# Cross-attention on one Trainium2 core: the output product with the output weights stationary and 512 tokens moving

## The chip, the cores and the metric

The kernel runs on one core of a Trainium2 chip, in one launch. The metric is device time in microseconds (us) of that launch: the median of three runs. The kernel's instructions go to five engines, each working through a queue of its own in the order in which the program writes them: PE (matrix products; its weight loads are listed as PEld), DVE (VectorE), ACT (ScalarE), POOL (GpSimd) and SP (SyncE), which here issues nearly all DMA transfers.

## The reference: what is computed

Inputs are x (32 batches, 512 tokens, 640 channels), a context of 32 x 77 x 1024, and weights. With 77 context tokens the object, other and image parts of the context are empty, so what is left is one cross attention with 20 heads of 32 channels, an output product, a bias and the residual:

```python
q = _heads(hidden_states @ to_q_w)                       # 32 x 20 x 512 x 32
h_txt = _sdpa(q, _heads(ehs_txt @ to_k_w), _heads(ehs_txt @ to_v_w))
out = _merge(h_txt)                                      # 32 x 512 x 640
out = out @ to_out_w + to_out_b
out = (out + residual) / RESCALE                         # residual = x, RESCALE = 1
```

All is float32. The kernel makes its big products in a rounded float32 form, each operand split into a high and a low part and three of the four partial products kept (PAIRS, line 113).

## The kernel before, in words

**Stages.** Up to about 250 us keys and values of all batches are computed from the context and written to scratch in device memory (lines 258 to 360). After that the kernel runs 160 *slots* (slot, line 588), one for each batch b and each chunk j of 128 channels (four heads): n = 5b + j. A slot has, among other work:

- scores(n): 32 small matmuls from qt (the queries, copied out of the bank pq) and kb (keys) into four banks sc, line 423;
- maxima(n) on DVE (line 435), exps(n) on ACT (line 445), normalize(n): a reciprocal on DVE (line 455) and a product on POOL (line 457), all on the probabilities pn;
- transpose_p(n - 1) on DVE (line 464), which turns pn in blocks of 32 into the tile z, and move_p, four DMAs on SP's queue that put z into raw with keys on the partitions (line 473). There are two buffers each of pn, z, qt and raw;
- queries(n + 1): 15 matmuls with wq_s stationary and 512 tokens moving (line 401), and copy_q, which puts the result into qt (line 410; on DVE in the slots below 7, on ACT from then on);
- values(m): 8 matmuls from raw and vb (line 483), then high_a on ACT (line 497) and low_a on DVE (line 502), which split the result into the tile at, one for each slot, eight buffers plus three borrowed ones;
- transpose_x on DVE (line 235) in chunks j = 0 and 1, two pieces each, and split_x on ACT and POOL (lines 245 and 246) in chunks 2 and 3, both for the next batch.

From slot 8 on (PAIRED) the slots differ by parity. An even slot, here called *paired*, computes values for two earlier slots at its end and issues a move_p behind them; an odd slot computes none, and issues its move_p in its middle, behind transpose_p. So two moves follow each other within a paired and the next unpaired slot.

**The output product.** For a batch, the projection goes over four blocks of 128 tokens (t), two halves of 320 output channels (h) and five chunks j: STEPS, 40 steps of three matmuls (project, line 521). The stationary operand is the piece at[tokens], 128 x 128, and the moving one is 320 columns of the output weights wo_s. Each (t, h) fills one PSUM bank po, which DVE adds onto the residual row tile xr (finish, line 550); there is one bank po. PIECES (line 565) spreads the steps of a batch over five slots, 7 to 10 steps in each: one part right after the scores, ahead of the queries, and one after the queries. The residual rows xr (128 tokens x 640 channels) are loaded by load_residual (line 509) and get the bias on POOL (add_bias, line 513); after both halves they go out (lines 554 and 556).

**The order.** manual_schedule (line 249) keeps, on each engine and on SP's queue, the order in which the program emits instructions; the framework adds waits where tiles are reused or read. An instruction that waits holds up everything behind it on its engine. In slot, for DVE, this order is: maxima, low_a, finish, transpose_p(n - 1), transpose_x, the reciprocal of normalize, finish. In the slots 1, 2, 5 and 6 transpose_p comes right behind maxima (line 606), and copy_q stands behind it on DVE (line 639); in the slots 3 and 4 transpose_p stands behind copy_q (line 640).

Of the kernel before, what the change touches and what calls it, by code (L numbers as in the profile page):

```python
# [23 lines left out]
P = 128  # L24
# [13 lines left out]
def kernel(  # L38
# [66 lines left out]

    def split_weights(dst, w, k, scale=None):
# [4 lines left out]
        split(dst[:, 0, :], dst[:, 1, :], part)  # L111

# [184 lines left out]
    def split_wo():  # L297
        k = len(split_ks) - NC_
        split_ks.append(k)
        ws = kvw.tile([P, 2, C], FPR, tag="ws", name="ws", bufs=2)  # L300
        split_weights(ws, wo, k)
        nc.sync.dma_start(wo_dram[:, k].bitcast(F32), ws.bitcast(F32))
# [73 lines left out]
    nc.sync.dma_start(bias, bo.unsqueeze(0).to_broadcast([P, C]))  # L376
    kbs = [main.tile([P, NC_, NKEY], F32, name=f"kb{n}") for n in range(2)]
# [31 lines left out]
    def copy_q(n, copy=nc.scalar.copy):  # L409
        copy(qts[n % 2], pqs.pop(n))  # L410

    def scores(n):
        b, j = divmod(n, NC_)
        scs[n] = [
            late[1].tile([P, NQ, P], F32, tag=LENT[n][i], name="sc", bufs=1 + (LENT[n][i] == "pa"))
            if i in LENT.get(n, ())
            else ps.tile([P, NQ, P], F32, tag="sc", name="sc", bufs=4)
            for i in range(HPC)
        ]
        for t in range(NQ):  # L420
            for i, sc in enumerate(scs[n]):
                r = slice(i * HD, (i + 1) * HD)
                nc.tensor.matmul(  # L423
                    sc[:, t, :NKEY],
                    qts[n % 2][r, t * P : (t + 1) * P],
                    kbs[b % 2][r, j, :],
                    start=True,
                    stop=True,
                    tile_position=(i * HD, 0),
                )  # L430
# [30 lines left out]
    def transpose_p(n):  # L461

        pn, z = pnb[n % 2], zs[n % 2]
        nc.vector.transpose(  # L464
            z.rearrange("p c h t j -> p (h t) c j"),
            pn.rearrange("p a (c i) -> p a c i", i=Q),
        )

    def move_p(n):

        raws[n] = late[0].tile([KPAD, NQ, HPC, P], F32, tag="raw", name="raw", bufs=2)
        for a in range(4):
            nc.sync.dma_start(  # L473
                raws[n][:, a].rearrange("p h q -> p (h q)"),
                zs[n % 2][a * Q : (a + 1) * Q].rearrange("i c h t j -> i c (h t j)"),
            )
# [15 lines left out]
    def high_a(n):  # L492
        if n % 11 < 8:
            at = late[0].tile([P, 2, S], FPR, tag="at", name="at", bufs=8)
        else:
# [9 lines left out]

    def load_residual(b, t, xr=None):
        if xr is None:
            xr = late[0].tile([P, C], F32, tag="xr", name="xr", bufs=4)
        nc.sync.dma_start(xr, x[b, t * P : (t + 1) * P, :])
        xrs[b, t] = xr  # L510

    def add_bias(b, t):
        nc.gpsimd.tensor_tensor(xrs[b, t], xrs[b, t], bias, ALU.add)  # L513

    def output_bank(b, t, h):
        if (b, h) == (B - 2, 0) and t > 0:
            pos[b, t, h] = ps.tile([P, S], F32, tag="pq", name="po", bufs=1)
        else:
            pos[b, t, h] = late[1].tile([P, S], F32, tag="po", name="po", bufs=1)

    def project(b, t, h, j):
        for m, (a, c) in enumerate(PAIRS):
            nc.tensor.matmul(  # L523
                pos[b, t, h][:, :HALF],
                ats[b * NC_ + j][:, a, t * P : (t + 1) * P],
                wos[0][:, j, c, h * HALF : (h + 1) * HALF],
                start=(j == 0 and m == 0),
                stop=(j == NC_ - 1 and m == 2),
            )

    STEPS = [(t, h, j) for t in range(NQ) for h in range(2) for j in range(NC_)]
    closed = []

    def piece(b, lo, hi):
        for t, h, j in STEPS[lo:hi]:
            if j == 0:
                output_bank(b, t, h)
            project(b, t, h, j)  # L540
            if j == NC_ - 1:
                closed.append((b, t, h))

    def finish():

        while closed:
            b, t, h = closed.pop(0)
            xr = xrs[b, t]
            cols = slice(h * HALF, (h + 1) * HALF)
            nc.vector.tensor_tensor(  # L550
                xr[:, cols], pos.pop((b, t, h))[:, :HALF], xr[:, cols], ALU.add
            )
            if (b, t) == (B - 1, NQ - 1):
                nc.sync.dma_start(out[b, t * P : (t + 1) * P, cols], xr[:, cols])
            elif h == 1:
                nc.sync.dma_start(out[b, t * P : (t + 1) * P, :], xr)

# [6 lines left out]

    PIECES = {
        2: ((2, 35, 40), (1, 0, 3)),
        3: ((1, 3, 5), (1, 5, 10)),
        4: ((1, 10, 15), (1, 15, 18)),
        0: ((2, 18, 20), (2, 20, 25)),
        1: ((2, 25, 30), (2, 30, 35)),  # L570
    }
    RESIDUAL = {1: (1, 0), 2: (1, 1), 4: (1, 2), 0: (2, 3)}
    BIAS = {2: (1, 0), 3: (1, 1), 0: (2, 2), 1: (2, 3)}
    TRANSPOSE_X = {0: (0, 1), 1: (2, 3)}
# [13 lines left out]
    def slot(n, beside=()):  # L588
        b, j = divmod(n, NC_)
        ahead, more = n + 1 < N, b + 1 < B  # L590
        pieces = [(b - back, lo, hi) for back, lo, hi in PIECES[j]]
        filling = n < NC_ + 2
# [23 lines left out]
        if b and j and b + 2 < B:  # L616
            load_x(b + 2, (j - 1,))
        if j in RESIDUAL and b >= RESIDUAL[j][0]:
            load_residual(b - RESIDUAL[j][0], RESIDUAL[j][1])
        if j in BIAS and b >= BIAS[j][0]:  # L620
            add_bias(b - BIAS[j][0], BIAS[j][1])
# [49 lines left out]
        if n == PAIRED - 1:  # L671
            move_p(n - 1)
        finish()
        if paired:
            move_p(n - 1)

    def end():


        last = B - 1  # L680
        load_residual(last - 1, 3)
        add_bias(last - 1, 2)
        add_bias(last - 1, 3)
        piece(last - 1, 18, 20)
        take(N - 3)
        finish()
        load_residual(last, 0)
        load_residual(last, 1)
        piece(last - 1, 20, 25)
        finish()  # L690
        transpose_p(N - 1)
        move_p(N - 1)
        piece(last - 1, 25, 30)
        finish()
        take(N - 2)
        piece(last - 1, 30, 35)
        finish()
        load_residual(last, 2)
        piece(last - 1, 35, 40)
        finish()  # L700
        for t in (0, 1, 2):
            add_bias(last, t)

        def begin(i, j0, j1):
            t, h = divmod(i, 2)
            if j0 == 0:
                if i < 4:
                    pos[last, t, h] = ps.tile([P, S], F32, tag="sc", name="po", bufs=4)
                elif i == 4:
                    pos[last, t, h] = ps.tile([P, S], F32, tag="pq", name="po", bufs=1)  # L710
                elif i == 5:
                    output_bank(last, t, h)
                else:
                    pos[last, t, h] = late[1].tile([P, S], F32, tag="pa", name="po", bufs=2)
            for j in range(j0, j1):
                project(last, t, h, j)

        for i in range(4):
            begin(i, 0, 4)
        take(N - 1)  # L720
        load_residual(last, 3)
        add_bias(last, 3)
        for i in (4, 5):
            begin(i, 0, 4)

        def close(t):
            for h in range(2):
                project(last, t, h, 4)
                closed.append((last, t, h))
            finish()  # L730

        close(0)
        close(1)
        begin(6, 0, 4)
        close(2)
        begin(7, 0, 4)
        close(3)
# [65 lines left out]
```

## Time and profile before

| what | value |
|---|---|
| time, median of 3 runs | 1742.69 us (1742.63 to 1742.89) |
| the profiled execution's own time | 1742.87 us |
| its span, first to last instruction | 1741.1 us |
| PE busy | 1732.8 us (100%) |
| DVE, ACT, POOL busy | 974.0, 1122.0, 788.9 us (56, 64, 45%) |
| time of the SP queue's packets, share of 16 DMA engines | 69.2% |
| granted TensorE clock | 1.0 |

The rows that the prediction shows come from one profiled execution. The page gives totals and the costliest groups of instructions (line, engine, operation, what it writes and reads, count, busy time, mean duration in ns, idle time before it). The timeline lists instructions in order of time with runs of the same kind merged: start, duration, engine, line, shapes, count, and in brackets the idle time of the engine before it with what ended it. A matmul's end is modelled, and matmuls overlap in the pipeline, so that spacing is read from one start to the next.

### The profile page before, as it was taken

What the parts mean: (1) busy time and instruction counts of PE and PEld (TensorE: products, weight loads), DVE (VectorE), ACT (ScalarE), POOL (GpSimd) and SP (SyncE); (2) the same over time, 40 slices, a digit from 0 to 9 for tenths busy, and PEclk for the clock granted to TensorE, in tenths of its full rate; (3) what the DMA queues carried; (4) which work ended last, traced back from release to release, by engine and by line L of the source; (5) the groups of instructions that cost most, each with busy time, mean ns of one, the idle gap of its engine ahead of it and who ended that gap; (6) DMA issues with size and microseconds to landing.
All of it is one profiled execution on the core that took longest, in us unless ns stands there. A gap on an engine that the chain in (4) does not pass through costs nothing.

```text
span 1741.1 us, 39488 instructions
## 1 busy us (share of the span) xinstructions
PE 1732.8 (100%) x13862; PEld 1434.1 (82%) x13862; DVE 974.0 (56%) x1651; ACT 1122.0 (64%) x5698; POOL 788.9 (45%) x502
## 2 busy tenths in 40 slices
PE   9999999999999999999999999999999999999999
PEld 7888898788888888888888888888888888888887
DVE  5342235656566565665666656656566566655653
ACT  3131126877777777777777777777777777777772
POOL 0000026555545545555455554555545555555443
PEclk9999999999999999999999999999999999999999
DMA  9847576877677676776776767767677677776655
GB/s 186 159 92 185 109 144 166 202 174 196 170 194 189 174 188 177 192 193 171 194 187 170 197 170 187 193 168 194 175 185 198 163 194 184 180 189 176 164 156 161
DMA packets 268567, 306.60 MB, mean 176 GB/s; under 512 B 88720, under 2 KB 165008, under 8 KB 268368
## 3 DMA queue, kind: packets, MB, share of 16 engines
q1 hardware_dynamic: 265776, 296.94, 69.2%
q0 software_dynamic: 2496, 6.97, 1.3%
q8 instruction: 110, 1.80, 0.4%
q14 instruction: 89, 0.73, 0.1%
q10 hardware_dynamic: 96, 0.16, 0.0%
HBM read 120.27 MB, written 57.88 MB: 102 GB/s over the span
## 4 chain that ended last, share of the span: by engine, by line
PE 98%; ACT 1%; DMA 1%; DVE 0%; issue 0%; SPq 0%; DVEq 0%; ACTq 0%
PE po L523 33%; PE pq L401 31%; PE sc L423 10%; PE pa L483 8%; PE pv L177 8%; PE pk L177 8%; DMA raw<-z 1%; ACT pn L445 1%; PE warm L256 0%; DVE z L464 0%; SPq L473 0%; DVE qt L410 0%; DVE nm L435 0%; DVE xr L550 0%; DVE zero L253 0%
## 5 line engine op out<-in xcount | busy, mean ns | idle before, releaser
L445 ACT ACTIVATE pn<-sc,nm 128x77 f32<-128x77 f32 x2560 | 788.1, 362 | 239.1 <-DVE nm L435 194.1
L457 POOL TENSOR_TENSOR pn<-pn,rs 128x1232 f32<-128x1232 f32 x160 | 363.4, 2271 | 689.1 <-DVE rs L455 682.8
L523 PE MATMUL po<-wo_s,at 128*128 128x320 f32 x3840 | 628.3, 313 | 0.0
L445 ACT ACTIVATION_READ_ACCUMULATOR pn<-sc,nm 128x1 f32 x2560 | 621.9, 243 | 0.0
L523 PEld LDWEIGHTS po<-wo_s,at 128*128 128x128 f32 x3840 | 575.3, 188 | 26.7 <-issue 2.5
L401 PE MATMUL pq<-xt,wq_s 128*128 128x512 f32 x2355 | 564.8, 391 | 0.0
L401 PEld LDWEIGHTS pq<-xt,wq_s 128*128 128x128 f32 x2355 | 435.4, 188 | 84.1
L435 DVE TENSOR_REDUCE nm<-sc 128x4 f32<-128x308 f32 x640 | 261.4, 471 | 137.0 <-PE sc L423 137.0
L464 DVE STREAM_TRANSPOSE z<-pn 128x1536 f32<-128x1536 f32 x160 | 283.0, 1769 | 0.7 <-DMA raw<-z 0.5
L423 PEld LDWEIGHTS sc<-kb,qt 32*128 32x128 f32 x5120 | 157.3, 186 | 85.4 <-ACT at L497 63.7
L550 DVE TENSOR_TENSOR xr<-po,xr 128x320 f32<-128x320 f32 x256 | 124.8, 489 | 167.8 <-PE po L523 146.5
L246 POOL TENSOR_TENSOR xt<-xs,xt 128x512 fp32r<-128x512 f32 x157 | 198.0, 1286 | 35.1 <-ACT xt L245 35.1
L513 POOL TENSOR_TENSOR xr<-xr,bias 128x640 f32<-128x640 f32 x128 | 200.4, 1566 | 13.2 <-DMA xr<-in_x_dram 11.1
L502 DVE TENSOR_TENSOR at<-pa,at 128x512 fp32r<-128x512 f32 x160 | 109.8, 686 | 148.2 <-ACT at L497 148.2
L497 ACT CAST at<-pa 128x512 fp32r<-128x512 f32 x160 | 94.1, 588 | 140.2 <-PE pa L483 138.9
L423 PE MATMUL sc<-kb,qt 32*128 32x77 f32 x5120 | 180.9, 277 | 2.2 <-DVE qt L410 1.4
L483 PE MATMUL pa<-raw,vb 96*32 96x512 f32 x1280 | 154.7, 599 | 0.8 <-DMA raw<-z 0.8
L177 PE MATMUL pv<-ct,wv_s 128*128 128x512 f32 (+1 forms) x600 | 133.9, 381 | 0.0
L177 PE MATMUL pk<-ct,wk_s 128*128 128x512 f32 (+1 forms) x600 | 133.4, 381 | 0.0
L177 PEld LDWEIGHTS pv<-ct,wv_s 128*128 128x128 f32 x600 | 112.5, 188 | 19.1
L177 PEld LDWEIGHTS pk<-ct,wk_s 128*128 128x128 f32 x600 | 112.4, 188 | 19.2 <-DVE wk_s L90 0.4
L410 ACT COPY qt<-pq 128x512 f32<-128x512 f32 x153 | 95.4, 623 | 31.1 <-PE pq L401 31.1
(35 smaller groups left out, 490.6 us busy)
## 6 DMA issues: line engine op xcount, KB each, us to landing
raw<-z SPq DMA_DIRECT2D x640, 192.0 KB, 3.5
xs<-in_x_dram SPq DMA_DIRECT2D x128, 320.0 KB, 5.3
xr<-in_x_dram SPq DMA_DIRECT2D x128, 320.0 KB, 5.0
out_dram<-xr SPq DMA_DIRECT2D x127, 320.0 KB, 4.2
vb<-v_dram SPq DMA_DIRECT2D x32, 240.0 KB, 4.6
kb<-k_dram SPq DMA_DIRECT2D x32, 192.5 KB, 3.9
cs<-in_ctx_dram SPq DMA_DIRECT2D x12, 512.0 KB, 9.3
k_dram<-ks POOLq DMA_DIRECT2D x20, 256.0 KB, 2.5
```

The source lines that it names most:

```text
L177: nc.tensor.matmul(held[j][:, :gn], w[:, k, a, :], cts[g, k][:, c, :gn], start=(k == 0 and n == 0), stop=(k == NK - 1 and n == 2),)
L246: low.tensor_tensor(parts[1], src, parts[0].bitcast(F32), ALU.subtract)
L401: nc.tensor.matmul(pqs[n], wq_s[:, k, a, j * P : (j + 1) * P], xts[b, k][:, c, :], start=(k == 0 and m == 0), stop=(k == NC_ - 1 and m == 2),)
L423: nc.tensor.matmul(sc[:, t, :NKEY], qts[n % 2][r, t * P : (t + 1) * P], kbs[b % 2][r, j, :], start=True, stop=True, tile_position=(i * HD, 0),
L435: nc.vector.tensor_reduce(nms[n][:, i], sc[:, :, :NKEY], AX.X, ALU.max, negate=True)
L445: nc.scalar.activation(pnb[n % 2][:, at, :NKEY], sc[:, t, :NKEY], AF.Exp, bias=nms[n][:, i, t : t + 1], accum_out=sms[n][:, at : at + 1],)
L457: nc.gpsimd.tensor_tensor(pf, pf, rs.unsqueeze(2).to_broadcast([P, NQ * HPC, NKEY]), ALU.mult)
L464: nc.vector.transpose(z.rearrange("p c h t j -> p (h t) c j"), pn.rearrange("p a (c i) -> p a c i", i=Q),)
L483: nc.tensor.matmul(pas[n][i * HD : (i + 1) * HD, :].rearrange("p (a q) -> p a q", q=P), vb[:, i, :], raw[:, :, i, :], start=True, stop=Tru ...
L513: nc.gpsimd.tensor_tensor(xrs[b, t], xrs[b, t], bias, ALU.add)
L523: nc.tensor.matmul(pos[b, t, h][:, :HALF], ats[b * NC_ + j][:, a, t * P : (t + 1) * P], wos[0][:, j, c, h * HALF : (h + 1) * HALF], start= ...
L550: nc.vector.tensor_tensor(xr[:, cols], pos.pop((b, t, h))[:, :HALF], xr[:, cols], ALU.add)
```

## The change

The output product of all batches but the last is turned round. Its stationary operand is a piece of wo_s, 128 x 128, and its moving operand is at with all 512 tokens (group). One group makes a block c of 128 output channels for 512 tokens: 15 matmuls of 512 columns in one whole bank. A batch has five groups, and GROUP puts one into each slot: nine matmuls after the scores, six after the queries. The columns of wo are permuted when it is split (turned=True), so that VectorE's transpose in blocks of 32 (turn) turns a bank into the layout in which x is loaded for the queries: partition = (channel quarter, token in 32), free = (token block, channel). POOL then adds the turned block ot onto the tile y (add). y holds x of a whole batch in that layout, loaded in quarters (load_y, LOAD_Y) and given the bias on POOL in four pieces (bias_of, with bias_y); two buffers. It goes out in the same layout, in pieces of 160 channels, that is 640 bytes (store_y, STORE_Y). The last batch keeps the old form on rows, with its own load_residual, project and finish.

For room, z and qt have one buffer instead of two, and at seven plus three instead of eight plus three. slot keeps its order otherwise. The core of the diff:

```diff
-    qts = [main.tile([P, S], F32, name=f"qt{n}") for n in range(2)]
-    zs = [main.tile([P, KBLK, HPC, NQ, Q], F32, name=f"z{n}") for n in range(2)]
+    qt = main.tile([P, S], F32, name="qt")
+    z = main.tile([P, KBLK, HPC, NQ, Q], F32, name="z")
...
+    def load_y(b, quarters):
+        if b not in ys:
+            ys[b] = late[0].tile([P, S // Q, U], F32, tag="y", name="y", bufs=2)
+        src = x[b].rearrange("(a j) (q u) -> q j a u", j=Q, q=4)
+        for q in quarters:
+            nc.sync.dma_start(ys[b][q * Q : (q + 1) * Q], src[q])
+
+    def bias_of(b, i):
+        part = ys[b][:, 4 * i : 4 * i + 4]
+        nc.gpsimd.tensor_tensor(
+            part, part, bias_y.unsqueeze(1).to_broadcast([P, 4, U]), ALU.add
+        )
+
+    def store_y(b, quarters):
+        dst = out[b].rearrange("(a j) (q u) -> q j a u", j=Q, q=4)
+        for q in quarters:
+            nc.sync.dma_start(dst[q], ys[b][q * Q : (q + 1) * Q])
...
+    def group(b, c, ks, tag="po"):
+
+        for k in ks:
+            if k == 0:
+                pos[b, c] = bank(tag)
+            for m, (a, d) in enumerate(PAIRS):
+                nc.tensor.matmul(
+                    pos[b, c],
+                    wos[0][:, k, a, c * P : (c + 1) * P],
+                    ats[b * NC_ + k][:, d, :],
+                    start=(k == 0 and m == 0),
+                    stop=(k == NC_ - 1 and m == 2),
+                )
+
+    def turn(b, c):
+        ots[b, c] = late[0].tile([P, S], F32, tag="ot", name="ot", bufs=1)
+        nc.vector.transpose(ots[b, c], pos.pop((b, c)))
+
+    def add(b, c):
+        part = ys[b][:, :, c * Q : (c + 1) * Q]
+        nc.gpsimd.tensor_tensor(
+            part, part, ots.pop((b, c)).rearrange("p (a i) -> p a i", i=Q), ALU.add
+        )
...
+    GROUP = {3: (1, 0), 4: (1, 1), 0: (2, 2), 1: (2, 3), 2: (2, 4)}
+    LOAD_Y = {0: (0,), 1: (1,), 2: (2, 3)}
+    BIAS = {4: (1, (0, 1)), 0: (2, (2,)), 1: (2, (3,))}
+    STORE_Y = {3: (0, 1), 4: (2, 3)}
...
-        if pieces[0][0] >= 0:
-            piece(*pieces[0])
+        if og >= 0:
+            group(og, oc, range(3))
         for i in range(2):
             exps(n, i)
-        finish()
         if not filling:
             transpose_p(n - 1)
         if n >= LATE and n != PAIRED - 1 and not paired and not copied:
             move_p(n - 1)
+        if j in STORE_Y and b > 1:
+            store_y(b - 2, STORE_Y[j])
...
-        if pieces[1][0] >= 0:
-            piece(*pieces[1])
+        if og >= 0:
+            group(og, oc, range(3, NC_))
+            turn(og, oc)
...
-        finish()
+        if og >= 0:
+            add(og, oc)
```

In end, the groups c = 2, 3 and 4 of the last batch but one are computed between the remaining values, two of them in the bank pq.

More of the change, by code (lines that the diff above doesn't have):

```diff
@@ L110, in split_weights @@
             nc.scalar.mul(part, part, scale)
-        split(dst[:, 0, :], dst[:, 1, :], part)
+        hi, lo = dst[:, 0, :], dst[:, 1, :]
+        if turned:
+            part = part.rearrange("p (q c i) -> p c q i", q=4, i=Q)
+            hi, lo = (d.rearrange("p (c q i) -> p c q i", q=4, i=Q) for d in (hi, lo))
+        split(hi, lo, part)
     PAIRS = ((0, 0), (0, 1), (1, 0))
@@ L376 @@
     nc.sync.dma_start(bias, bo.unsqueeze(0).to_broadcast([P, C]))
+    U = C // 4
+    bias_y = main.tile([P, U], F32, name="bias_y")
+    for q in range(4):
+        nc.sync.dma_start(
+            bias_y[q * Q : (q + 1) * Q, :],
+            bo[q * U : (q + 1) * U].unsqueeze(0).to_broadcast([Q, U]),
+        )
     kbs = [main.tile([P, NC_, NKEY], F32, name=f"kb{n}") for n in range(2)]
@@ L461, in transpose_p @@
     def transpose_p(n):
[L463 removed]
+        pn = pnb[n % 2]
         nc.vector.transpose(
@@ L504, in low_a @@
         )
[L506 to L528, printed above, removed]
-            )
[L533 to L556, printed above, removed]
+    ys, ots = {}, {}
@@ new lines, in bank @@
+    def bank(tag):
+        pool, bufs = (ps, {"sc": 4, "pq": 1}[tag]) if tag in ("sc", "pq") else (late[1], {"po": 1, "pa": 2}[tag])
+        return pool.tile([P, S], F32, tag=tag, name="po", bufs=bufs)
+    def group(b, c, ks, tag="po"):
[10 more added lines that the diff above has]
+                )
@@ new lines, in turn, with load_residual @@
+    def turn(b, c):
[5 more added lines that the diff above has]
+            part, part, ots.pop((b, c)).rearrange("p (a i) -> p a i", i=Q), ALU.add
+        )
+    def load_residual(t):
+        if B - 1 not in ys:
+            ys[B - 1] = late[0].tile([P, S // Q, U], F32, tag="y", name="y", bufs=2)
+        rows = ys[B - 1].rearrange("p a u -> p (a u)")
+        xrs[t] = rows[:, t * C : (t + 1) * C]
+        nc.sync.dma_start(xrs[t], x[B - 1, t * P : (t + 1) * P, :])
@@ new lines, in add_bias, with project @@
+    def add_bias(t):
+        nc.gpsimd.tensor_tensor(xrs[t], xrs[t], bias, ALU.add)
+    def project(t, h, k):
+        for m, (a, d) in enumerate(PAIRS):
+            w = wos[0][:, k, d].rearrange("p (c w) -> p c w", c=NC_)
+            nc.tensor.matmul(
+                pos[t, h][:, :HALF].rearrange("p (c w) -> p c w", c=NC_),
+                ats[(B - 1) * NC_ + k][:, a, t * P : (t + 1) * P],
+                w[:, :, 2 * h * Q : 2 * (h + 1) * Q],
+                start=(k == 0 and m == 0),
+                stop=(k == NC_ - 1 and m == 2),
+            )
@@ new lines, in finish @@
+    def finish(t, h):
+        xr, last = xrs[t], B - 1
+        part = xr.rearrange("p (q c i) -> p c q i", q=4, i=Q)[:, :, 2 * h : 2 * h + 2]
+        got = pos.pop((t, h))[:, :HALF].rearrange("p (c q i) -> p c q i", q=2, i=Q)
+        nc.vector.tensor_tensor(part, got, part, ALU.add)
+        rows, cols = slice(t * P, (t + 1) * P), slice(h * HALF, (h + 1) * HALF)
+        if t == NQ - 1:
+            nc.sync.dma_start(out[last, rows, cols], xr[:, cols])
+        elif h == 1:
+            nc.sync.dma_start(out[last, rows, :], xr)
@@ L590, in slot @@
         ahead, more = n + 1 < N, b + 1 < B
-        pieces = [(b - back, lo, hi) for back, lo, hi in PIECES[j]]
+        og, oc = b - GROUP[j][0], GROUP[j][1]
         filling = n < NC_ + 2
@@ L617, in slot @@
             load_x(b + 2, (j - 1,))
[L618 to L619 removed]
+        if j in LOAD_Y and 0 < b < B:
+            load_y(b - 1, LOAD_Y[j])
         if j in BIAS and b >= BIAS[j][0]:
[L621 to L623 removed]
+            for i in BIAS[j][1]:
+                bias_of(b - BIAS[j][0], i)
+        if og >= 0:
+            group(og, oc, range(3))
         for i in range(2):
             exps(n, i)
[L626 removed]
         if not filling:
@@ L680, in end @@
         last = B - 1
[L681 to L684, printed above, removed]
+        for t in range(3):
+            load_residual(t)
         take(N - 3)
[L686 to L690, printed above, removed]
+        group(last - 1, 2, range(NC_), "pq")
+        turn(last - 1, 2)
+        bias_of(last - 1, 2)
+        add(last - 1, 2)
         transpose_p(N - 1)
@@ L692, in end @@
         move_p(N - 1)
-        piece(last - 1, 25, 30)
-        finish()
-        take(N - 2)
[L696 to L704, printed above, removed]
-            t, h = divmod(i, 2)
[L706 to L724, printed above, removed]
+        load_residual(3)
+        group(last - 1, 3, range(NC_))
+        turn(last - 1, 3)
+        bias_of(last - 1, 3)
+        add(last - 1, 3)
+        take(N - 2)
+        group(last - 1, 4, range(NC_), "pq")
+        turn(last - 1, 4)
+        add(last - 1, 4)
+        store_y(last - 1, range(4))
+        for t in range(NQ):
+            add_bias(t)
@@ L726, in close, with begin @@
+        def begin(i):
+            t, h = divmod(i, 2)
+            pos[t, h] = bank(("sc", "sc", "sc", "sc", "po", "pq", "pa", "pa")[i])
+            for k in range(4):
+                project(t, h, k)
         def close(t):
             for h in range(2):
-                project(last, t, h, 4)
-                closed.append((last, t, h))
-            finish()
+                project(t, h, 4)
+                finish(t, h)
+        for i in range(4):
+            begin(i)
+        take(N - 1)
@@ L732, in end @@
+        for i in (4, 5):
+            begin(i)
         close(0)
         close(1)
-        begin(6, 0, 4)
+        begin(6)
         close(2)
-        begin(7, 0, 4)
+        begin(7)
         close(3)
```

23 lines of the change are left out of this document (7 added, 16 removed).

## The prediction

> **What bounds the kernel now.** I read the page first: busy times, the chain that ended last, the costliest groups.
>
> ```profile
> span 1741.1 us, 39488 instructions
> PE 1732.8 (100%) x13862; PEld 1434.1 (82%) x13862; DVE 974.0 (56%) x1651; ACT 1122.0 (64%) x5698; POOL 788.9 (45%) x502
> PE 98%; ACT 1%; DMA 1%; DVE 0%; issue 0%; SPq 0%; DVEq 0%; ACTq 0%
> L523 PE MATMUL po<-wo_s,at 128*128 128x320 f32 x3840 | 628.3, 313 | 0.0
> L401 PE MATMUL pq<-xt,wq_s 128*128 128x512 f32 x2355 | 564.8, 391 | 0.0
> L457 POOL TENSOR_TENSOR pn<-pn,rs 128x1232 f32<-128x1232 f32 x160 | 363.4, 2271 | 689.1 <-DVE rs L455 682.8
> L246 POOL TENSOR_TENSOR xt<-xs,xt 128x512 fp32r<-128x512 f32 x157 | 198.0, 1286 | 35.1 <-ACT xt L245 35.1
> ```
>
> PE is the bound: whatever makes it wait adds to the time in full, whatever shortens its work is won in full. Its busy time per matmul (628.3/3840 = 0.164 us at 320 columns, 564.8/2355 = 0.240 at 512) holds the ends of pieces, which overlap the next. So I take starts from the timeline, first an odd slot of chunk 1:
>
> ```profile
> 1080.18 1.13 PE L423 MATMUL sc<-kb,qt 32*128 32x77 f32 x32
> 1081.24 2.47 PE L523 MATMUL po<-wo_s,at 128*128 128x320 f32 x15
> 1083.55 3.60 PE L401 MATMUL pq<-xt,wq_s 128*128 128x512 f32 x15
> 1086.98 2.36 PE L523 MATMUL po<-wo_s,at 128*128 128x320 f32 x15
> 1089.27 1.13 PE L423 MATMUL sc<-kb,qt 32*128 32x77 f32 x32
> ```
>
> then the end of an odd slot of chunk 2, with a shorter second piece:
>
> ```profile
> 1051.40 1.48 PE L523 MATMUL po<-wo_s,at 128*128 128x320 f32 x9
> 1052.81 1.13 PE L423 MATMUL sc<-kb,qt 32*128 32x77 f32 x32
> ```
>
> The 15 queries take 3.43 us, **0.2287** each. Second pieces of 15 and 9 take 2.29 and 1.41: six more cost 0.88, so **0.1467** each, plus 0.09 for the piece. The first piece after the scores (2.31) has 0.11 of its own. Nothing stands idle between these pieces.
>
> **The change, part by part.** *The matmuls.* A batch has 120 of 320 columns = 17.60 us; after it 75 of 512, the form of the queries, = 17.15. The columns streamed are the same 38400; 45 matmuls' fixed cost goes, **0.45 us a batch**. Pieces per slot stay two, so their own cost stays. Slots 8 to 158 are 30.2 batches: **-13.6 us**. The busy times would give 1.65 a batch, -50 us, but hold ends that the change doesn't remove. I keep -10 to -19 as its bounds.
>
> An odd slot becomes 1.06 (scores) + 2.17 (nine) + 3.43 + 1.46 (six) = 8.12 us, and the next group wants the bank po 9.18 after this slot's scores began.
>
> *DVE and POOL loads.*
>
> ```profile
> L210 DVE STREAM_TRANSPOSE vs<-pv 128x512 f32<-128x512 f32 x20 | 14.1, 711 | 104.2 <-PE pv L177 104.2
> L550 DVE TENSOR_TENSOR xr<-po,xr 128x320 f32<-128x320 f32 x256 | 124.8, 489 | 167.8 <-PE po L523 146.5 <-POOL xt L246 15.3 <-issue 3.5
> ```
>
> Eight adds of 0.489 (3.9 a batch) become five turns; L210 is the same turn, PSUM to SBUF, 512 columns: 0.711, together 3.6. POOL gets five adds of 512 elements, like L246: 1.29 each; the bias has as many elements as before. POOL has then 2.27 + 1.29 (add) + 1.29 (split) + about 1.3 (bias) = 6.1 of a mean slot of 9 us: hidden. Only where split_x of chunk 3 follows a late normalize might it reach the next queries: 0 to 3 us in all, taken as **+1**.
>
> *One z instead of two.* This adds a wait: transpose_p(n - 1) must now wait until move_p(n - 2) has read z. DVE and the moves, in the odd slot above and one other:
>
> ```profile
> 1084.15 1.77 DVE L464 STREAM_TRANSPOSE z<-pn 128x1536 f32<-128x1536 f32 x1
> 1085.85 1.53 DVE L235 STREAM_TRANSPOSE xs<-xs 128x640 f32<-128x640 f32 x2
> 1087.30 0.21 DVE L455 RECIPROCAL rs<-sm 128x16 f32<-128x16 f32 x1
> ```
> ```profile
> 1079.45 2.63 SPq L473 DMA_DIRECT2D raw<-z  x4
> ```
> ```profile
> L473 SPq DMA_DIRECT2D raw<-z x4: 590/593/712, 1079.5 to 1081.4; - x4
> DMA to landing us min/median/max: 2.7/3.3/3.8
> ```
> ```profile
> L473 SPq DMA_DIRECT2D raw<-z x4: 577/593/728, 1025.2 to 1027.1; - x4
> DMA to landing us min/median/max: 2.7/4.2/4.9
> ```
>
> The paired slot's move starts 0.73 us before the odd slot's scores and can't start earlier, since it waits for raw. Its last DMA lands at 1081.4 + 3.8, that is 5.0 after the scores began; in the other slot 1027.1 - 1025.2 - 0.73 + 4.9 = 6.1. The transpose started at 3.97 there: it comes 1 to 2 us later. Behind it on DVE stand, in chunks 0 and 1, transpose_x, the reciprocal, and now turn, which frees po. With DVE's start 0.21 after a landing and PE's 0.05 after DVE (rows below), the bank is free at L + 0.21 + 3.15 (transpose to reciprocal, 1084.15 to 1087.30) + 0.21 + 0.71 + 0.05 = L + 4.33. PE wants it at 9.18, so it waits L - 4.85: 0.15 us for L = 5.0, 1.25 for 6.1. I take 0.5, nearer to the first. The program has 29 such odd slots: **+14.5 us** (4 to 36). In chunks 2 to 4 the 1.5 us of transpose_x are not there and turn is ready as the six matmuls end; turn 0.1 + 0.71 + 0.05 after them still meets the 1.06 us of the scores: nothing. In even slots, values' two microseconds cover it: the odd slot's move lands 5.7 us (1.9 of issues, 3.8) after its transpose ends at 7, that is 13, the next transpose ends by 15, and SP wants it at 17.3. With qt, copy_q writes long after the scores have read it: nothing.
>
> *The same wait where the slots are short.* In slots 1 to 6, copy_q is on DVE too, and PE's scores wait for it.
>
> ```profile
> 287.80 1.77 DVE L464 STREAM_TRANSPOSE z<-pn 128x1536 f32<-128x1536 f32 x1
> 289.88 0.69 DVE L410 COPY qt<-pq 128x512 f32<-128x512 f32 x1 [0.31 <-PE pq L401]
> ...
> 296.05 1.77 DVE L464 STREAM_TRANSPOSE z<-pn 128x1536 f32<-128x1536 f32 x1
> ...
> 306.36 1.78 DVE L464 STREAM_TRANSPOSE z<-pn 128x1536 f32<-128x1536 f32 x1 [0.53 <-DMA raw<-z]
> ```
> ```profile
> L473 SPq DMA_DIRECT2D raw<-z x4: 607/740/1557, 285.2 to 288.1; - x4
> DMA to landing us min/median/max: 3.9/4.5/5.5
> ```
> ```profile
> 290.62 1.13 PE L423 MATMUL sc<-kb,qt 32*128 32x77 f32 x32 [0.78 <-DVE qt L410]
> ...
> 308.86 1.13 PE L423 MATMUL sc<-kb,qt 32*128 32x77 f32 x32 [0.61 <-DVE qt L410]
> ...
> 314.62 1.13 PE L423 MATMUL sc<-kb,qt 32*128 32x77 f32 x32
> ...
> 322.80 1.13 PE L423 MATMUL sc<-kb,qt 32*128 32x77 f32 x32 [0.84 <-ACT qt L410]
> ```
> ```profile
> 299.78 6.37 DMA raw<-z
> ```
>
> The last row is of the chain in order of time: the DMA ended at 306.15 and DVE started at 306.36, 0.21 later; 289.88 + 0.69 against 290.62 gives PE's 0.05. The row at 306.36 also shows that even two buffers of z made DVE wait here once. Now slot 2: move_p(0) lands at about 293.0 (288.1 + 4.5 to 5.5), so the transpose of 287.80 goes at 293.2, copy_q ends at 295.7, the scores of 290.62 start 5.1 us late. Slot 3's transpose (296.05) is late by the same 5.1, and ends at 302.9. From there each transpose follows the one before by 1.77 + 5.7 + 0.21 = 7.7 us, where slots took about 6: 308.8, 316.5, 324.2. The scores of 308.86 come at 319.0, those of 314.62 at 326.7, 12.1 late. Slot 7 loses nine output matmuls that stood in it, I give back 1: **+11 us** (5, the first wait alone, to 16, with the last row's 6.4 us to landing instead of 3.8). PE never gets it back, since it is the bound from slot 8 on.
>
> *DMA.* x and the output move in pieces of 640 bytes instead of 2560.
>
> ```profile
> xs<-in_x_dram SPq DMA_DIRECT2D x128, 320.0 KB, 5.3
> xr<-in_x_dram SPq DMA_DIRECT2D x128, 320.0 KB, 5.0
> ```
>
> xs has those pieces already, xr not; they land almost alike, and the number of issues on SP stays. load_y waits for the stores of its buffer, with only a later move behind it. I take nothing, and price it as a rival.
>
> *The end.*
>
> ```profile
> 1702.13 4.67 PE L523 MATMUL po<-wo_s,at 128*128 128x320 f32 x30
> 1706.73 1.07 PE L483 MATMUL pa<-raw,vb 96*32 96x512 f32 x8
> ```
>
> Before, 30 matmuls cover the landing of the raw that values needs. One group now (3.4 us) ends at 1705.6, where raw lands near 1706.1 (5.0 after scores at 1701.07): 0.5. Sixty groups' matmuls (13.7) replace 90 (13.2): 0.5. With 0.5 for a second late move I take **+1.5** (0 to 4).
>
> **The sum** goes against the profiled execution's own 1742.87 us (span 1741.1), 0.2 above the median of 1742.69: -13.6 + 1 + 14.5 + 11 + 1.5 = +14.4, so **1757 us**.
>
> **Rivals.**
>
> - *The clock falls.* In slots 2 and 5 PE would stand still 5 to 7 us.
>
> ```profile
> L256 PE MATMUL warm<-zero 128*128 128x512 f32 x22 | 8.1, 547 | 1.5 <-DVE zero L253 1.5
> ```
>
>   The first 22 matmuls of the launch take 8.1 us where 22 x 0.2287 are 5.0: a cold start costs up to 3.1. Two more of them, the second partly inside a wait for z, add about 4: 1761. Against it: nothing but that the waits of PE shown here are under 1 us, so that no row decides. The Trainium skill, "TensorE: Matmul & The Clock Gate", section "Why this matters for your kernels", says that a pause of more than about 3 us between matmuls drops the clock to half; by that rule this is what happens. The trace shows the slow start, and no fall in mid-run.
> - *Small pieces slow the moves* (slower by more). If every move lands 1 us later, the 29 slots pay 1 more each and the short slots 4: 1757 + 33 = 1790. For it: more packets on a queue with 69% of the engines' time. Against it: xs beside xr.
> - *The two sizes cancel.* All landings as in the better slot (0.15 x 29 = 4), 8 in the short slots, nothing else: 1741.
> - *The other side, faster:* z's wait is covered wherever DVE has slack. It decides at L = 4.85 in the odd slots and, in the short ones, if moves take 4.5 us instead of 5.7, so that only the first wait counts: -13.6 + 5.1 + 1 = 1735. For it: one of the two slots has 5.0. Against it: the row at 306.36.
>
> **How the numbers follow.** Forecast (1757) 0.43, clock 0.20, small pieces 0.15, cancelling 0.12, faster 0.10. A measurement of this kernel can tell about 0.2%, 3.5 us, from no change: 1739.2 to 1746.2. The forecast's own low end (0.04) reaches below 1746, so faster 0.10, same 0.16, slower 0.74. The range 1740 to 1782 leaves out the faster case and the upper half of the small pieces.
>
> **What would show it.** Right: matmuls of the group 0.229 us apart; DVE's transpose into z waiting for raw<-z in most odd slots; PE waiting for DVE's turn at the first group matmul only behind odd slots of chunks 0 and 1; scores of slot 8 some 11 us later than 322.80. Wrong: scores of slot 3 still near 290.6, landings of moves below 4.85 or above 6.1 as a rule, or PE waiting on POOL.

## The result and the profile after

The changed kernel takes **1771.06 us**, the median of four runs (1768.15 to 1772.28), against 1742.66 us (1742.43 to 1742.89) of the kernel before on the same chip: a ratio of **1.0161**, 95% interval 1.0143 to 1.0178. The forecast was 1757, and the range 1740 to 1782 holds the result. The profiled execution took 1770.29 us with a span of 1768.5, 27.4 more than before's 1741.1. The page of the changed kernel, first the totals and the chain that ended last, then three groups (line, engine, operation, count, busy us, mean ns, idle time before and what ended it):

```profile
span 1768.5 us, 36481 instructions
PE 1733.0 (98%) x12467; PEld 1319.4 (75%) x12467; DVE 965.1 (55%) x1558; ACT 1128.9 (64%) x5698; POOL 985.1 (56%) x657
PE 84%; DMA 7%; DVE 4%; SPq 3%; issue 2%; ACT 0%; POOL 0%; DVEq 0%; ACTq 0%; POOLq 0%
L549 PE MATMUL po<-at,wo_s 128*128 128x512 f32 x2325 | 604.9, 401 | 21.2 <-DVE ot L559 21.0
L563 POOL TENSOR_TENSOR y<-y,ot 128x512 f32<-128x512 f32 x155 | 199.8, 1289 | 2.6 <-DVE ot L559 2.4
L559 DVE STREAM_TRANSPOSE ot<-po 128x512 f32<-128x512 f32 x155 | 108.1, 698 | 105.1 <-PE po L549 100.5
```

PE's share of the chain fell from 98 to 84%. The 14 points that it lost stand under DMA, DVE, SP's queue and issue: the end is now set in part by transfers and by what waits for them, although PE's busy sum is the same (1732.8 before); after the change that sum holds stretches at half clock, below. The turn takes 698 ns, where 711 were reckoned. The view of waits (total us, times, longest) names them:

```profile
POOL pn L470 <- DVE rs L468: 511.1, 130, 8.0
DVE z L477 <- DMA raw<-z: 313.0, 131, 4.4
PE po L549 <- DVE ot L559: 21.0, 21, 2.5
PE sc L436 <- DVE rs L468: 5.8, 1, 5.8
```

The row with the largest total costs nothing: POOL is not the bound. The second costs only where it reaches PE, and the last two rows are where it does: 21 waits for the turn, and one in the short slots.

To find the 27.4 us I laid the start of every slot's scores of the two traces side by side. Up to slot 0: +0.8 us. Slots 0 to 8: +6.7. Slots 8 to 159: +19.5, the difference of the lengths, 1397.80 and 1378.27, in these two rows (a stretch, its length, busy time of the engines, granted clock, DMA share, GB/s; the first row is of the kernel after, the second of before):

```profile
330.31:1728.11 1397.80, 1376.45 (x10579) 1023.28 (x10579) 821.40 (x1327) 1012.43 (x5285) 904.52 (x572) 1.00 0.80 179
```
```profile
322.80:1701.07 1378.27, 1378.27 (x11934) 1135.98 (x11934) 829.60 (x1416) 1005.67 (x5285) 716.31 (x423) 1.00 0.72 182
```

The end: 40.40 us against 40.03, +0.4. In the long stretch PE was never idle before; after, 21.35 us of it are.

**Slots 8 to 159.** One pair of slots of the changed kernel in the timeline, first PE (start, duration, idle time before in brackets), then DVE, then SP's queue:

```profile
450.50 1.13 PE L436 MATMUL sc<-kb,qt 32*128 32x77 f32 x32
451.56 2.34 PE L549 MATMUL po<-at,wo_s 128*128 128x512 f32 x9
453.73 3.57 PE L414 MATMUL pq<-xt,wq_s 128*128 128x512 f32 x15
457.14 1.55 PE L549 MATMUL po<-at,wo_s 128*128 128x512 f32 x6
458.62 1.13 PE L436 MATMUL sc<-kb,qt 32*128 32x77 f32 x32
461.23 2.33 PE L549 MATMUL po<-at,wo_s 128*128 128x512 f32 x9 [1.48 <-DVE ot L559]
```
```profile
457.24 1.78 DVE L477 STREAM_TRANSPOSE z<-pn 128x1536 f32<-128x1536 f32 x1 [3.37 <-DMA raw<-z]
458.94 1.53 DVE L239 STREAM_TRANSPOSE xs<-xs 128x640 f32<-128x640 f32 x2
460.39 0.21 DVE L468 RECIPROCAL rs<-sm 128x16 f32<-128x16 f32 x1
460.53 0.65 DVE L559 STREAM_TRANSPOSE ot<-po 128x512 f32<-128x512 f32 x1
```
```profile
448.16 0.32 SPq L526 DMA_DIRECT2D y<-in_x_dram  x1
449.77 2.67 SPq L486 DMA_DIRECT2D raw<-z  x4
```

The odd slot from 450.50 to 458.62 lasts 8.12 us, as the prediction had it. The six matmuls close the bank at about 458.6, but DVE is inside the chain of transposes that began late, and the turn starts at 460.53. PE has run its 1.06 us of scores and then stands 1.48 us. Such a wait falls into the next, paired slot. If no slot waited, 75 odd slots of 8.13 and 76 paired ones of 9.97 would take 1367.5 us, **10.8 less** than before took. The other **30.3 us** are waits, and matmuls slowed behind them: 7.8 in paired slots of chunk 1 (behind an odd slot of chunk 0), **18.8** in paired slots of chunk 2 (behind an odd slot of chunk 1), 3.7 in all the rest.

**Slots 0 to 8.** DVE and PE of the changed kernel, of DVE the transposes into z from slot 2 on and one copy_q, of PE the scores of the slots 3, 6 and 8:

```profile
288.57 1.77 DVE L477 STREAM_TRANSPOSE z<-pn 128x1536 f32<-128x1536 f32 x1
...
304.15 1.78 DVE L477 STREAM_TRANSPOSE z<-pn 128x1536 f32<-128x1536 f32 x1 [1.55 <-DMA raw<-z]
311.89 1.78 DVE L477 STREAM_TRANSPOSE z<-pn 128x1536 f32<-128x1536 f32 x1 [3.74 <-DMA raw<-z]
313.59 0.65 DVE L423 COPY qt<-pq 128x512 f32<-128x512 f32 x1
319.68 1.78 DVE L477 STREAM_TRANSPOSE z<-pn 128x1536 f32<-128x1536 f32 x1 [1.07 <-DMA raw<-z]
```
```profile
291.40 1.13 PE L436 MATMUL sc<-kb,qt 32*128 32x77 f32 x32 [0.79 <-DVE qt L423]
...
314.39 2.00 PE L436 MATMUL sc<-kb,qt 32*128 32x77 f32 x32 [5.81 <-DVE rs L468]
330.31 1.75 PE L436 MATMUL sc<-kb,qt 32*128 32x77 f32 x32 [1.67 <-ACT qt L423]
```

The first transpose shown does not wait, and the scores of slot 3 come at 291.40, 0.78 after before's 290.62. The next ones wait for the moves, 7.74 and 7.79 us apart. The one of 311.89 holds up copy_q (313.59), and PE stands 5.81 us ahead of slot 6; the releaser that the row names, the reciprocal, is DVE's neighbour of that copy. The scores of 314.39 take 2.00 instead of 1.13 us, because the clock fell. In the windows of the two stretches, the third number from the end is the granted clock, 0.96 and then 0.64:

```profile
302.80:314.39 11.59, 5.78 (x60) 3.91 (x56) 6.50 (x10) 7.31 (x44) 2.27 (x1) 0.96 0.55 126
314.39:322.84 8.45, 8.45 (x55) 6.07 (x55) 4.87 (x9) 5.01 (x32) 2.27 (x1) 0.64 0.94 199
```

### The profile page after: what moved, and what is told of

It reads as the page before. It is cut to its first block, busy times and chain, and to the rows that moved or that the text cites. A ratio compares the mean times of both kernels' runs of the same rounds, so it can differ in the third digit from the quotient of the medians.

```text
span 1768.5 us, 36481 instructions
## 1 busy us (share of the span) xinstructions
PE 1733.0 (98%) x12467; PEld 1319.4 (75%) x12467; DVE 965.1 (55%) x1558; ACT 1128.9 (64%) x5698; POOL 985.1 (56%) x657
## 4 chain that ended last, share of the span: by engine, by line
PE 84%; DMA 7%; DVE 4%; SPq 3%; issue 2%; ACT 0%; POOL 0%; DVEq 0%; ACTq 0%; POOLq 0%
PE po L549 28%; PE pq L414 27%; PE pa L496 7%; PE sc L436 7%; PE pv L181 7%; PE pk L181 7%; DMA raw<-z 5%; SPq L486 2%; DVE z L477 1%; DVE xs L239 1%; DMA wraw<-in_L_xattn_to_k_w_dram 1%; PE po L581 1%; DVE ot L559 1%; DMA y<-in_x_dram 0%; SPq L99 0%
## 5 line engine op out<-in xcount | busy, mean ns | idle before, releaser
L549 PE MATMUL po<-at,wo_s 128*128 128x512 f32 x2325 | 604.9, 401 | 21.2 <-DVE ot L559 21.0
L549 PEld LDWEIGHTS po<-at,wo_s 128*128 128x128 f32 x2325 | 426.5, 189 | 123.3 <-DVE ot L559 24.7
L414 PEld LDWEIGHTS pq<-xt,wq_s 128*128 128x128 f32 x2355 | 444.2, 189 | 95.4 <-POOL xt L250 0.8
L563 POOL TENSOR_TENSOR y<-y,ot 128x512 f32<-128x512 f32 x155 | 199.8, 1289 | 2.6 <-DVE ot L559 2.4
L530 POOL TENSOR_TENSOR y<-y,bias_y 128x640 f32<-128x640 f32 x124 | 193.4, 1571 | 7.3
L559 DVE STREAM_TRANSPOSE ot<-po 128x512 f32<-128x512 f32 x155 | 108.1, 698 | 105.1 <-PE po L549 100.5
```

The lines of the kernel that those rows point to most:

```text
L414: nc.tensor.matmul(pqs[n], wq_s[:, k, a, j * P : (j + 1) * P], xts[b, k][:, c, :], start=(k == 0 and m == 0), stop=(k == NC_ - 1 and m == 2),)
L530: nc.gpsimd.tensor_tensor(part, part, bias_y.unsqueeze(1).to_broadcast([P, 4, U]), ALU.add)
L549: nc.tensor.matmul(pos[b, c], wos[0][:, k, a, c * P : (c + 1) * P], ats[b * NC_ + k][:, d, :], start=(k == 0 and m == 0), stop=(k == NC_ - ...
L563: nc.gpsimd.tensor_tensor(part, part, ots.pop((b, c)).rearrange("p (a i) -> p a i", i=Q), ALU.add)
```

## The experiments

The theory behind all of them is that the single z is what costs: its transpose waits for the move ahead of it, and what stands behind it on DVE (the turn in the long stretch, copy_q in the short slots) arrives late at PE. The rivals set against it put the loss elsewhere: with smaller pieces of DMA, with POOL's added work, or with the new order of the transfers. Ratios are to the kernel before, run on the same chip.

**e1_turn_first.** The turn no longer stands behind x's transposes.

```diff
-        if not filling:
-            for i in turns:
-                transpose_x(b + 1, i)
...
             group(og, oc, range(3, NC_))
             turn(og, oc)
+        if not filling:
+            for i in turns:
+                transpose_x(b + 1, i)
```

> The changed kernel with one move: on VectorE, the two transpose_x of chunks 0 and 1 stand behind turn instead of ahead of it. Theory A (the one buffer z: in odd slots of chunks 0 and 1 VectorE starts late, and turn, which frees the bank po, is held up behind transpose_x): the waits of PE for turn shrink from about 27 us to about 5, those with a move over 6.3 us after the scores; 1771 - 22 = 1749 us. Rival B (the 640-byte pieces slow every transfer, and PE loses at several places): the moves land as late as before and the time falls by less than half of that, 1760 or more. Rival C (POOL's added work comes late and holds up the next transpose): the order of transpose_x and turn does not matter, 1768 to 1774.

Measured: 1746.59 us (1743.98 to 1750.69, ten runs), ratio 1.0021 (1.0012 to 1.003). That is 24.5 us less than the changed kernel, with no transfer and no operation of POOL removed. In its waits

```profile
PE po L549 <- DVE ot L559: 3.7, 6, 1.5
```

and the extra time of the paired slots of chunks 1 and 2 is 0.2 and 3.8 us instead of 7.8 and 18.8. So 22.6 of these 26.6 us come from the turn's place behind z's late transpose and transpose_x.

**e2_y_later.** The first two quarters of y are loaded together in chunk 1, none in chunk 0.

```diff
-    LOAD_Y = {0: (0,), 1: (1,), 2: (2, 3)}
+    LOAD_Y = {1: (0, 1), 2: (2, 3)}
```

> The changed kernel with LOAD_Y as {1: (0, 1), 2: (2, 3)}: the first quarter of y is loaded in chunk 1 and no longer in chunk 0. Theory A, with this addition: in chunk 0 load_y waits on SP for the stores of its buffer, goes out just ahead of the paired slot's move, and shares the engines with it, which is why the move ahead of an odd chunk 1 lands 6.1 us after the scores on average where it was 5.4. Then the move is back at 5.4 and the paired chunk 2, which loses 19 us behind it, loses about 9: 1761 us. Rival B (all moves are slower through the sheer number of 640-byte packets): the landing stays at 6 and the time at 1768 to 1774.

Measured: 1753.36 us (1751.88 to 1758.41, four runs), ratio 1.0069 (1.0052 to 1.0086): 17.7 us less than the changed kernel, more than was expected. The waits for the turn halve:

```profile
PE po L549 <- DVE ot L559: 10.4, 18, 1.6
```

The extra time of chunk 2's paired slots goes from 18.8 to 5.4, that of chunk 1's from 7.8 only to 5.7. The edit takes one transfer from ahead of the move that an odd slot of chunk 1 waits for. Its last DMA landed 6.11 us after the scores began on the mean in the changed kernel (14 slots, all but the first), here 5.42, and before 5.43. The pieces of 640 bytes are all still there: as such they do not slow the moves. The place of one load does. The kernel before also loaded a quarter in chunk 0, in pieces of 2560 bytes and some 7.6 us ahead of this move; whether larger pieces would cost as much at the late place, no run shows.

**e3_before_one_z.** The kernel before, with nothing changed but z.

```diff
-    zs = [main.tile([P, KBLK, HPC, NQ, Q], F32, name=f"z{n}") for n in range(2)]
+    zs = [main.tile([P, KBLK, HPC, NQ, Q], F32, name="z")] * 2
```

> The kernel before with one buffer z instead of two and nothing else of the change; rows, 2560-byte pieces and two buffers qt stay. Theory A: the wait alone costs most of what the change lost. In the short slots the first move is as late as in the kernel before, so slot 3 is 5 us late and slot 8 some 11 to 15; odd slots of chunk 0, where the addition onto xr stands behind transpose_x, lose about 0.6 each (8 us), those of chunk 1, which are longer, 1 to 2 us in all: 1742.7 + 13 + 10 = 1766 us. Rival B: without the small pieces the odd slots lose almost nothing and only the short slots remain, 1754 to 1757. If z has nothing to do with it, 1743.

Measured: 1768.73 us (1768.25 to 1768.96, four runs), ratio 1.0147 (1.0132 to 1.0163). One buffer of z taken from the old kernel costs nearly what the whole change does. It costs it in other places, though:

```profile
PE sc L423 <- DVE qt L410: 11.4, 2, 5.7
...
PE po L523 <- DVE xr L550: 5.7, 10, 1.2
```

Both waits of 5.7 us stand in the short slots, ahead of slots 3 and 6; its slot 8 comes 14.5 us later than before, the long stretch adds 9.3 and the end 2.2. Of the 9.3, 5.6 come behind odd slots of chunk 0, 0.3 behind those of chunk 1, and 3.4 behind those of chunk 3, which the expectation did not name. So it is by chance that the two totals are alike. What the run shows is that one z alone makes PE wait.

**e4_copy_first.** In slots 5 and 6 too, copy_q stands ahead of z's transpose on DVE.

```diff
-        copied = n in (3, 4)
+        copied = 3 <= n <= 6
```

> The changed kernel with copied = 3 <= n <= 6 for n in (3, 4): in slots 5 and 6 as well, copy_q stands ahead of transpose_p on VectorE, so that the scores of slots 6 and 7 do not wait behind a transpose that waits for z. Theory A: slot 8 starts at about 324 instead of 330.3, no pause of over 5 us on PE is left, the granted clock stays 1.00 there, and the time falls by 5 to 7: 1765 us. Rival (the short slots are bound by the moves themselves, whatever the order): slot 8 stays near 330 and the time at 1769 to 1772.

Measured: 1768.2 us (1765.41 to 1771.06, four runs), ratio 1.0145 (1.013 to 1.016): 2.9 less than the changed kernel, which the spread of the two hardly tells from nothing, where 5 to 7 were expected of the theory that copy_q's place is what costs there. Slot 8 starts at 327.65, neither at 324 nor near 330; with the short slots unchanged it started at 328.80 to 330.31 (the changed kernel, e1, e2 and e7). The granted clock falls there as before. The transposes come as far apart as ever (first fence), and a part of PE's pause has moved to the values, which read raw (second fence):

```profile
303.60 1.78 DVE L477 STREAM_TRANSPOSE z<-pn 128x1536 f32<-128x1536 f32 x1 [1.52 <-DMA raw<-z]
311.41 1.78 DVE L477 STREAM_TRANSPOSE z<-pn 128x1536 f32<-128x1536 f32 x1 [3.22 <-DMA raw<-z]
319.16 1.78 DVE L477 STREAM_TRANSPOSE z<-pn 128x1536 f32<-128x1536 f32 x1 [3.16 <-DMA raw<-z]
```
```profile
315.51 1.94 PE L496 MATMUL pa<-raw,vb 96*32 96x512 f32 x8 [2.17 <-issue]
```

So the short slots are bound by the chain of transpose and move itself, 7.8 us a link. This order on DVE does not mend that; whether a second z does is e6's question.

**e5_both_orders.** The edits of e1 and e2 together.

> The changed kernel with both edits of e1 and e2: transpose_x behind turn, and the first quarter of y loaded in chunk 1. Theory A: what e1 left of the waits for turn (4 us behind odd chunk 1) goes down to under 1, the short slots lose what they lost: 1742 us, the time of the kernel before, since the PE work saved (11) then only pays for the short slots (7) and the small rest. If the two edits worked through one another and not through turn, the sum of both, 1729; if the landing of the moves still matters, 1746 as in e1.

Measured: 1744.64 us (1741.12 to 1746.05, eleven runs), ratio 1.0004 (0.9995 to 1.0013): no difference from the kernel before. The waits for the turn are gone:

```profile
PE po L549 <- DVE ot L559: 0.8, 4, 0.2
```

In its profiled execution (1741.29 us, the second lowest of the eleven) slots 8 to 159 take 1369.62 us, 8.7 less than before: the gain of the turned product shows at last. The short slots, which end 6.2 us late (328.97 against 322.80), give most of it back.

**e6_spare_z.** Besides, a second z in the slots below 8, in the buffer of y that is empty until then.

```diff
+    spare = []
+
+    def z_of(n):
+        if n >= PAIRED or n % 2 == 0:
+            return z
...
+            part = late[0].tile([P, S // Q, U], F32, tag="y", name="spare", bufs=2)
...
-            z.rearrange("p c h t j -> p (h t) c j"),
+            z_of(n).rearrange("p c h t j -> p (h t) c j"),
```

> e5 with a second z in the short slots only: odd n below 8 use the room of the y buffer that is still empty then. Theory A: slot 8 starts near 322 instead of 330, no pause of PE over 1 us is left between slots 2 and 8, the granted clock stays 1.00, and the time is 1742 - 8 = 1734 us, faster than both kernels. Rival (the short slots are bound by the landing of the moves, also with two buffers): 1739 to 1742.

Measured: **1737.47 us** (1736.95 to 1738.54, five runs), ratio 0.9968 (0.9956 to 0.9981): 5.8 us under the kernel before beside it (median 1743.3 on that chip), and faster than both. The scores of the short slots:

```profile
308.73 1.13 PE L436 MATMUL sc<-kb,qt 32*128 32x77 f32 x32 [0.81 <-DVE qt L423]
314.49 1.13 PE L436 MATMUL sc<-kb,qt 32*128 32x77 f32 x32
322.94 1.13 PE L436 MATMUL sc<-kb,qt 32*128 32x77 f32 x32 [2.66 <-ACT qt L423]
324.00 3.70 PE L562 MATMUL po<-at,wo_s 128*128 128x512 f32 x9
```

They come within 0.2 us of before's (308.86, 314.62, 322.80). The 1734 us of the expectation were missed by 3.5: a pause of 2.66 us is left, ahead of slot 8, and the nine matmuls behind it take 3.70 us instead of 2.34, since the granted clock is 0.50 from 324.63 to 328.05.

**e7_no_add.** The changed kernel without POOL's add.

```diff
-        nc.gpsimd.tensor_tensor(
-            part, part, ots.pop((b, c)).rearrange("p (a i) -> p a i", i=Q), ALU.add
-        )
+        ots.pop((b, c))
```

> The changed kernel without POOL's add: the product is left out of the output, turn still runs. Theory A: POOL is not what holds up VectorE, the waits for turn stay, 1768 to 1772 us. Rival C (POOL comes late with normalize behind its added work, and the next transpose with it): the waits behind odd chunks 0 and 1 fall by half or more, under 1758.

Measured: 1770.21 us (1765.08 to 1772.34, four runs), ratio 1.0145 (1.013 to 1.0161), where the changed kernel has 1.0161. The waits are there as before:

```profile
PE po L549 <- DVE ot L559: 24.3, 20, 3.5
```

POOL's 199.8 us of adds cost no time that these runs can tell.

## Why the prediction was right, and where it was not

The direction and the mechanism were right: PE's work got shorter by some 10 us, and the single z gave back more. The sum of +14.4 stands against a measured +27.4 (spans of the profiled executions; the medians are 28.4 apart), so that the change cost nearly twice what was forecast:

| term | predicted us | measured us |
|---|---|---|
| matmuls of 512 columns, slots 8 to 158 | -13.6 | -10.8 |
| odd slots of chunks 0 and 1, turn behind z's wait | +14.5 | +26.6 |
| other slots from 8 on, split_x of chunk 3 among them | +1 | +3.7 |
| short slots, with the start of slot 0 | +11 | +7.5 |
| the end | +1.5 | +0.4 |

- *The matmuls.* The odd slot of 8.12 us came out at 8.13. Per slot a gain of 0.09 us was forecast (0.45 us over five). Odd slots went from a mean of 8.21 us to 8.13, a gain of 0.08. Paired ones went from 10.04 to 9.97, only 0.06, and there lie some 2 of the 2.8 us that are short of 13.6; why they gained less is not shown. The bounds of -10 to -19 held it.
- *The odd slots* are the **term that was mis-sized**: 0.5 us for each of 29, measured 26.6/29 = 0.9. The formula was sound: the pair shown above has its transpose at 457.24, 6.74 after its scores, so L = 6.53 with the 0.21 us behind a landing; L - 4.85 gives 1.68, and PE waited 1.48. What failed is L. It was taken from before's rows, nearer to their 5.0 than to their 6.1, and load_y, said to have "only a later move behind it", was put at nothing. In chunk 0 it has a paired slot's move behind it. SP holds the load back until the stores of its buffer have landed, 20 times in the whole run (first row below), and no such row is left in e2. The y load of 448.16 so goes out 1.61 us ahead of that move, and it lands 4.1 us later, at 452.2 (last row), 2.4 us after the move began:

```profile
SPq L526 <- DMA out_dram<-y: 36.1, 20, 2.7
```
```profile
L526 SPq DMA_DIRECT2D y<-in_x_dram x1: 323/323/323, 448.2 to 448.2; - x1
DMA to landing us min/median/max: 4.1/4.1/4.1
```

  In 14 of the 15 odd slots of chunk 1, all but the first, such a load was still under way for 2.4 to 4.5 us of the move; before and in e2, no load of x issued ahead of the move was. In 11 of the 14, SP issued the move 0.73 us ahead of the scores, as before, so that there it was slow under way and not late. In the other three the load went out only 0.43 us ahead of the move and SP issued the move 0.24 to 0.52 us later than that; these three lost 10.7 us. e2 takes the load away: a mean landing of 5.42 instead of 6.11, and 13.4 us less extra time behind these slots. Odd slots of chunk 0, which have no such load, had 5.43 (before 5.24) and lost 7.8 us in 14 slots, 0.6 each and near the 0.5 that was forecast; behind the 15 of chunk 1 it was 18.8/15 = 1.3. Some 4.8 of the 26.6 are not the wait but the half clock behind it, 1.6 in each of three slots.
- *Where the waits would be.* Right in the main: 18 of the 21 waits for the turn, 19.8 of their 21.0 us, come behind odd slots of chunks 0 and 1, and none behind a paired slot. Three short ones (0.17, 0.50 and 0.53 us) come behind odd slots of the chunks 2 and 4, where nothing was expected. e1 shows the cause by putting the turn ahead of transpose_x.
- *The short slots.* Here a **step failed**. The first wait of 5.1 us, ahead of slot 3, did not come, since move_p(0) was earlier. The prediction had named scores of slot 3 still near 290.6 as a sign of being wrong, and they came at 291.40, later only by the 0.8 us of slot 0. SP's row of the changed kernel, and then that of before:

```profile
276.68 3.08 SPq L486 DMA_DIRECT2D raw<-z  x4
```
```profile
285.20 3.78 SPq L473 DMA_DIRECT2D raw<-z  x4
```

  The prediction took 285.20 as given. By the order of the allocations, raw's place there no longer waits for tiles of the context stage; that is argued, and no run tests it. Where the old layout is kept, in e3, the wait came at 5.7 us and slot 3 was 5.2 late, so the step was right for z alone. The second step, 7.7 us from transpose to transpose, held (7.74, 7.79), and e4 and e6 show it to be the bound. That the term came out as near as 7.5 to 11 is in part luck: without the first wait the same sum gives 5.9, where the slots 0 to 8 lost 6.7. The start of slot 0 was 0.8 us late, which the prediction did not have.
- *The clock falls* was a rival at +4, for two falls in the short slots. One of these came, 0.64 behind the pause of 5.81 us, and four more stretches from slot 8 on (below), where they cost some 1.6 us each. These 6.4 us, 1.6 of them in the row of the other slots, are half of the 13 us by which the sum was short; they don't explain the sign, as the waits alone do more than eat the gain.
- *Small pieces slow the moves*: not as such (e2); at the late place it was not tried with larger ones. *POOL as the bound*: no (e7). *The end*: 0.4 is within 0 to 4.
- *The other side* was reached by the very term that I set against it: with z's wait off PE's path (e5), the kernel is level, and with a spare z in the short slots (e6) 0.3% faster.

## What to carry to other kernels

A buffer taken away costs where the wait for it meets an engine's order: ask what stands behind the waiting instruction, and put first what the bound engine needs next (e1: 24.5 us for moving a block of three lines). When a gain per step is a tenth of a microsecond and a wait hangs on a landing, follow each transfer that goes out just ahead of that one, whatever buffer it is for. And a filling phase has a bound of its own, which a buffer that is still empty there can lift (e6: 7.2 us below e5).

## What the runs showed of the hardware

**The clock falls after short pauses too.** In two successive slots of the changed kernel's timeline, nine matmuls behind a pause of 2.47 us take 3.02 us instead of 2.34; the second fence is a window, with a clock of 0.50 in the 3.41 us from 648.10 on:

```profile
635.99 2.34 PE L549 MATMUL po<-at,wo_s 128*128 128x512 f32 x9
...
646.65 3.02 PE L549 MATMUL po<-at,wo_s 128*128 128x512 f32 x9 [2.47 <-DVE ot L559]
```
```profile
648.10:651.51 3.41, 3.41 (x9) 2.64 (x9) 1.29 (x2) 3.41 (x24) 1.50 (x2) 0.50 1.01 244
```

Between the first scores and the last matmuls the trace has five such stretches at half clock, one of 6.8 us and four of 3.4, and they begin a whole number of 3.41 us apart (313.6, 330.6, 648.1, 962.1 and 1573.1: 5, 93, 92 and 179 times; the six of e4 are 4, 38, 55, 81 and 55 times apart). So the clock seems to be set in steps of 3.41 us. Pauses of 5.81, 2.47, 2.28, 1.67 and 1.63 us were followed by one; a pause of 2.48, of which about 1.0 and 1.5 lie on the two sides of a boundary between such steps, was not, nor were two of 1.48. In e4 two pauses of 1.3 us were, and one of 1.60 was not, so that a fixed bound is not to be had from these runs. The Trainium skill, "TensorE: Matmul & The Clock Gate", section "Why this matters for your kernels", advises against pauses of more than about 3 us between matmuls. Behind the 5.81 us the trace agrees; the half clock behind 1.63 to 2.47 us is below that figure, and here the measurement decides. The five stretches, 20.5 us at half clock, hold back some 10 us of PE's work at full clock, not all of it on the path.

**The spread from run to run goes with the clock.** The kernel before keeps within 1.8 us over 13 runs, at a mean granted clock of 1.0 (once 0.999, in the longest run). The changed one keeps within 4.1 over four (0.992 to 0.994), e1 within 6.7 over ten (0.995 to 0.998). In e5 four runs have a clock of 0.998 and a mean of 1742.5 us, the other seven 0.996 and 1744.8. e3 waits for landings as well, but has 0.995 in all four runs and keeps within 0.7. So a part of the spread seems to be how often half clock follows a pause. That is read from times and clocks side by side and not shown by an experiment; what makes the pauses differ from run to run stays open.
